# The other items' results of an attention and mixture-of-experts kernel: by blocks of 128 tokens in place of half items

## The chip, the cores and the metric

The kernel runs on one core of a Trainium2 chip. The metric is the device time of one execution in microseconds; the median of three executions of the kernel before is 2456.7 us (2454.43, 2456.7 and 2459.62). One more execution was recorded with the hardware profiler: it took 2459.43 us, of which the profile shows a span of 2457.7 us. All line numbers and rows are of that execution.

The engines are named as the profile names them: PE (TensorE, matrix products and transposes), PEld (its loads of weights), DVE (VectorE), ACT (ScalarE), POOL (GpSimd; here it issues the indirect DMAs that gather and scatter rows), SP (SyncE; here it issues the plain DMAs). Each engine takes its instructions in order, and waits on semaphores for those of others.

## The reference

The input is x of 8 items, each 256 channels by 1024 positions (32 by 32), float32. Two layers follow each other.

- Layer 0, on tokens (1024 by 256 in an item): `qkv = xt @ w_qkv + b_qkv`, 8 heads of 64, `attn = softmax(q k^T * 64**-0.5)` over the queries, `res = attn v`, then `res @ w_out + b_out + xt`.
- Layer 1: `t = t + attention(ln(t))` with one head and one matrix, `scores = (x W^T) x^T`, `y = softmax(scores) x`; then `t = t + moe(ln(t))`.
- The mixture of experts: `probs = softmax(tokens @ router_w.T)`, the two largest of 8 are kept and scaled to the sum 1, `out = tokens + sum over e of combine[:, e] * (gelu(tokens @ w1[e] + b1[e]) @ w2[e] + b2[e])`.

The result goes back to the layout of x: channels by positions.

## The kernel before

**The order of the whole.** Items 0 to 7 are computed one after the other. P is 128, D is 256, and an item has NT = 8 blocks of 128 tokens. Items 0 to 6 each go through layer 0, `attend` (the attention of layer 1), `normed` (the second layer norm and the router's products) and `dispatch`, which scatters each token's row to the places of its two experts; the item's tokens t2, with the norm already added to them, are stored to `sums` in memory. Before an item ends, the loads and first products of the next item's layer 0 are filled into its waits (`begun.at`). When layer 0 of item 7 is done, `experts` runs all experts' rows of items 0 to 6 in 63 blocks of 256 rows and writes the results to `y` in memory. What is left then is item 7 itself, and the collecting of the other seven items' results. The two are woven into each other, and this is the part that the change touches.

**Item 7.** `attend` runs eight steps, one for each block of 128 tokens: on PE the scores ps (L633, 128 by 1024), on DVE the negated maximum nmax (L641), on ACT the exponentials ex (L644), on PE eight transposes pa (L652), on DVE the copy aT (L654), on PE the product py (L659), on DVE L664, which scales py and adds it to t. The scores of later blocks are computed ahead. `normed` follows: layer norm on DVE (L217 to L224), transposes pt_n on PE (L233), copies n2T on DVE (L234), on POOL the addition of the norm to t (L775), and on PE the router's products pl (L687). Then `dense` computes all 8 experts for all tokens of item 7, since with one item there is nothing to sort: 16 steps, each with products pdh (L1164) and pdy (L1188) and the additions of pdy to t on DVE (L1197); the experts' weights come by plain DMAs (L1114, L1118).

**The results of items 0 to 6** (class `Results`). Each token has two rows in `y`, one for each of its experts. For an item and a half of its blocks (a "portion", 14 in all), eight indirect DMAs on POOL (L1053) fetch 128 rows of 256 numbers each into a tile yk; there are two such tiles, which share the tag xT. The item's `sums` are loaded into a tile o by SP (L1080). Eight instructions on DVE (L1085, `scalar_tensor_tensor`: row times gate plus o) add them. When an item's two halves are added, `store` transposes o on PE (pout, L1102, 8 for each of two channel halves of 128), copies each half on ACT to a tile oT (L1104), and SP writes it to the output (L1105).

**The places of that work.** The order on each engine is the order in which the program issues instructions, moved by a scheduler within what the dependences allow; `tc.issue_after(mixed.ins)` puts what follows behind the named DVE instruction. One `step()` is the whole of a portion: the store of an item that is complete, eight additions in a row, and the release of the eight gathers of the portion after next, which can start when DVE has read the yk tile that they overwrite. Two portions are begun ahead of `attend`. Which step of item 7 carries how many such steps is a table in the main loop, for the eight blocks of `attend` and the sixteen steps of `dense`:

```
early = {1: 1, 2: 1, 3: 1, 5: 1, 6: 1, 7: 1}
late = {0: 2, 3: 1, 4: 1, 6: 1, 8: 1, 9: 1, 11: 1, 12: 1}
```

In the changed kernel the same lines stand a few lines further on: L664 becomes L666, L654 L656, L641 L643, L687 L688, L775 L776; the gathers are at L1093, the additions at L1115, pout at L1152, oT at L1154, pdh at L1214 and pdy at L1238.

## Time and profile before

| | |
|---|---|
| times of three executions | 2454.43, 2456.7, 2459.62 us |
| the profiled execution | 2459.43 us, span 2457.7 us |
| PE busy | 97% of the span |
| DVE, ACT, POOL busy | 61%, 39%, 16% |
| chain of work that ended last | PE 90%, DVE 3%, ACT 2%, issue 2%, DMA 1%, another core or an unknown queue 1% |
| attention of an item (first L618 to end of last L664) | items 0 to 6 74.93 us each, item 7 105.6 us |
| from there to the first pl | items 0 to 6 8.02 us, item 7 8.96 us |
| gathers of results (L1053) | 112, mean 1048 ns, from 2193.6 us to 2419.4 us |
| additions of results (L1085) | 112, median 480 ns, 2226.7 to 2428.6 us |

How to read the rows. A group's line names its line in the program, the engine, the operation, the output and inputs by their names in the program, their sizes and the number of instructions, then the busy time, the mean of one, and the idle time of the engine just before them with what ended most of it. In a list in order of time the first two numbers are the start and the duration in us, and a bracket holds the idle time before it and what released it. "issue" stands for time in which the engine waited for nothing that the profile shows, "remote" for a release that the profile can't put down to an engine of this core. The busy time of matrix products is modelled at their ends. The clock is that which TensorE was granted, 1.00 being full speed. Matrix products in a row overlap, so a row's end can lie up to 0.2 us behind the next row's start.

### The profile page before, as it was taken

The page shows a single profiled execution, that of the slowest core. Times are in us where ns is not written, and L with a number is a line of the kernel's source. Part 1 is how long each engine was busy: PE and PEld are TensorE (multiplying, and loading weights), DVE is VectorE, ACT ScalarE, POOL GpSimd, SP SyncE. Part 2 cuts the span into 40 slices and gives each one's busy share as a digit, 9 for nine tenths or more (in the row PEclk, how much of TensorE's full clock was granted, in tenths as well). Part 3 has the DMA queues.
Part 4 walks back from the last instruction along what each step waited for, and adds up shares of the span by engine and source line. Part 5 has one row for each costly group of instructions (what it writes and reads, how often), then busy time and mean ns, then how long its engine had stood idle before and what let it go on. Part 6 is the DMA issues. An engine that isn't in the chain of part 4 may idle for free.

```text
span 2457.7 us, 37143 instructions
## 1 busy us (share of the span) xinstructions
PE 2386.2 (97%) x14015; PEld 1323.8 (54%) x14015; DVE 1497.3 (61%) x3642; ACT 953.5 (39%) x1587; POOL 391.1 (16%) x383
## 2 busy tenths in 40 slices
PE   9999999999999999999999999999999999997798
PEld 3356435654465346534653466346633788874466
DVE  5674677557746775577557755775578643334443
ACT  3651365136613661266126612662166222211222
POOL 0000011001100110011000100010002244444461
PEclk9999999999999999999999999999999999998799
DMA  7993101000100000000000000000002366652362
GB/s 280 386 376 83 35 18 36 1 18 19 35 1 18 19 19 17 18 16 21 18 18 14 23 18 18 10 27 1 18 7 74 116 208 223 208 173 91 99 196 91
DMA packets 82556, 188.23 MB, mean 77 GB/s; under 512 B 13992, under 2 KB 23880, under 8 KB 80584
## 3 DMA queue, kind: packets, MB, share of 16 engines
q1 hardware_dynamic: 57368, 118.65, 13.4%
q0 software_dynamic: 25008, 67.20, 8.7%
q8 instruction: 111, 1.82, 0.3%
q14 instruction: 69, 0.57, 0.1%
HBM read 100.49 MB, written 110.90 MB: 86 GB/s over the span
## 4 chain that ended last, share of the span: by engine, by line
PE 90%; DVE 3%; ACT 2%; issue 2%; DMA 1%; another core or an unknown queue 1%; SPq 0%; ACTq 0%; DVEq 0%; POOLq 0%
PE psc L420 18%; PE po L497 18%; PE py L659 9%; PE ps L633 7%; PE pqk L322 7%; PE pr L599 4%; PE pv L359 4%; PE ph L981 4%; PE pe L1006 4%; PE pdy L1188 2%; PE pdh L1164 2%; PE px L618 2%; PE pqk L300 2%; PE pa L652 2%
## 5 line engine op out<-in xcount | busy, mean ns | idle before, releaser
L461 ACT ACTIVATE ex<-psc,nmax 128x1024 f32<-128x1024 f32 x512 | 570.5, 1115 | 304.3 <-DVE scrap L444 221.8
L420 PE MATMUL psc<-qk,qk 64*64 64x512 f32 x4096 | 574.7, 592 | 4.3 <-ACT ex L461 4.3
L497 PE MATMUL po<-ex,vs 64*64 64x512 f32 x4096 | 570.2, 591 | 3.8 <-DVE vs L477 3.0
L444 DVE TENSOR_SCALAR_CACHE_REDUCE scrap<-psc,nmax 128x512 f32<-128x512 f32 x512 | 384.5, 751 | 178.4 <-PE psc L420 151.3
L435 DVE TENSOR_REDUCE nmax<-psc 128x1 f32<-128x512 f32 x512 | 350.8, 685 | 9.3 <-PE psc L420 9.3
L420 PEld LDWEIGHTS psc<-qk,qk 64*64 64x64 f32 x4096 | 179.8, 132 | 279.9 <-ACT ex L461 133.0
L497 PEld LDWEIGHTS po<-ex,vs 64*64 64x64 f32 x4096 | 175.3, 132 | 273.4 <-DVE vs L477 80.3
L659 PE MATMUL py<-n,aT 128*128 128x256 f32 x1024 | 244.4, 393 | 19.0 <-DVE aT L654 14.9
L659 PEld LDWEIGHTS py<-n,aT 128*128 128x128 f32 x1024 | 195.9, 195 | 84.5 <-DVE aT L654 53.8
L633 PE MATMUL ps<-nT,xa 128*128 128x512 f32 x512 | 236.5, 592 | 0.0
L844 POOL DMA_INDIRECT rows<-n,d_at x112 | 109.2, 975 | 705.5 <-DVE nmax L435 703.0
L644 ACT ACTIVATE ex<-ps,nmax 128x1024 f32<-128x1024 f32 x64 | 71.3, 1115 | 354.4 <-DVE nmax L641 338.6
L775 POOL TENSOR_TENSOR t<-t,n 128x2048 f32<-128x2048 f32 x8 | 36.3, 4535 | 1031.8 <-issue 766.8
L664 DVE SCALAR_TENSOR_TENSOR t<-py,rs,t 128x256 f32<-128x256 f32 x64 | 31.0, 484 | 234.9 <-PE py L659 197.8
L322 PE MATMUL pqk<-xT,wqkv 128*128 128x512 f32 x384 | 171.2, 599 | 0.0
L1053 POOL DMA_INDIRECT yk<-y,yat x112 | 117.4, 1048 | 120.9 <-DVE o L1085 72.2
L633 PEld LDWEIGHTS ps<-nT,xa 128*128 128x128 f32 x512 | 93.6, 190 | 79.9 <-issue 73.6
L322 PEld LDWEIGHTS pqk<-xT,wqkv 128*128 128x128 f32 x384 | 71.0, 190 | 99.9 <-issue 77.8
L287 ACT ACTIVATE qk<-pqk,b_qks 128x512 f32<-128x512 f32 x124 | 85.6, 691 | 96.1 <-PE pqk L322 79.8
L359 PE MATMUL pv<-wqkv,xT 128*128 128x512 f32 x256 | 119.6, 596 | 0.1
L641 DVE TENSOR_REDUCE nmax<-ps 128x1 f32<-128x1024 f32 x64 | 78.3, 1224 | 59.1 <-PE ps L633 58.6
L599 PE MATMUL pr<-wo,res 128*128 128x256 f32 x512 | 111.8, 379 | 0.0
(193 smaller groups left out, 2494.1 us busy)
## 6 DMA issues: line engine op xcount, KB each, us to landing
rows<-wb SPq DMA_DIRECT2D x7, 8192.0 KB
y<-yb SPq DMA_DIRECT2D x63, 256.0 KB
xT<-in_x_dram SPq DMA_DIRECT2D x7, 1024.0 KB
sums<-t SPq DMA_DIRECT2D x7, 1024.0 KB
o<-sums SPq DMA_DIRECT2D x7, 1024.0 KB
out_dram<-oT SPq DMA_DIRECT2D x14, 512.0 KB
wpack<-in_L_ffn_w_dram SPq DMA_DIRECT2D x4, 1024.0 KB
wb<-in_L_ffn_w_dram SPq DMA_DIRECT2D x16, 256.0 KB
```

Of the source, the lines that this page charges most:

```text
L322: mm = nc.tensor.matmul(pq[:, ts(n, 512)], wqkv[:, cc, t, ts(g, P)], xT[:, cc, ts(n, 512)], start=(cc == 0), stop=(cc == NCC - 1),)
L359: nc.tensor.matmul(pv, self.xT[:, cc, ts(i, P)], wqkv[:, cc, 2, :], start=(cc == 0), stop=(cc == NCC - 1),)
L420: mm = nc.tensor.matmul(pss[at, h][ts(c, DK), ts(n, 512)], k[r, j * P + c * DK : j * P + (c + 1) * DK], q[r, ts(n, 512)], start=True, stop ...
L435: firsts[at, h] = nc.vector.tensor_reduce(nmax, pss[at, h][:, ts(0, 512)], AX.X, ALU.max, negate=True)
L444: seconds[h] = nc.vector.tensor_scalar(scrap, pss[at, h][:, ts(1, 512)], -1.0, nmaxes[at, h], ALU.mult, ALU.min, accum_out=nmax,)
L461: nc.scalar.activation(ex, pss.pop((at, h)), AF.Exp, bias=nmaxes.pop((at, h)), scale=1.0, accum_out=sums[at][:, h : h + 1],)
L497: mm = nc.tensor.matmul(po[n][ts(h, DK), :], vss[at][keys, h, :], exps[at, h][keys, ts(n, 512)], start=(j == 0 and turn == 0), stop=(j == ...
L599: nc.tensor.matmul(pr[:, :C], res[:, g, ts(i, P)], wo[:, g, :], start=(g == 0), stop=(g == NPAIR - 1))
L633: nc.tensor.matmul(psc[:, ts(n, 512)], xa[:, ec, ts(i, P)], nT[:, ec, ts(n, 512)], start=(ec == 0), stop=(ec == NCC - 1),)
L659: nc.tensor.matmul(py[:, :D], aT[:, ts(m, P)], n1[:, m, :], start=(m == 0), stop=(m == NT - 1))
L844: scatter = nc.gpsimd.indirect_dma_start(out=view[:, :], out_offset=bass.IndirectOffsetOnAxis(ap=ats[k][:, i : i + 1], axis=0), in_=n2[:, ...
L1053: nc.gpsimd.indirect_dma_start(out=yk[:, i, k, :], out_offset=None, in_=self.group.y[:, :], in_offset=bass.IndirectOffsetOnAxis(ap=ats[k][ ...
```

## The change

The unit of the collecting becomes one block of 128 tokens: two gathers and two additions; there are 56 units. The two yk tiles are allocated once and used as a ring of eight slots, a unit in each. A table PLACES says for many more places of item 7 how many units are added there, how many are let go to POOL, and how many channel halves are stored. The places are DVE instructions of `attend` (the copies xa, the maxima, L666), `normed`, the gates and the steps of `dense`. A unit that is let go gets a dependence on the DVE instruction of its place ("behind"), so that POOL waits for it. A unit is added some two places after it is let go. In `attend` 22 of the 56 units are added, three at most places; none is added at the last block. A store is one channel half. The tiles o hold two items, and the next item's sums are loaded when the second block of an item is added. The counts of gathers, additions, loads of sums, transposes, copies and output DMAs stay what they are.

As the scheduler places them, five additions stand between L666 and the next copy aT, and a sixth behind the copy; the addition on POOL (L776) stands behind 60 of the 112 gathers; the four channel halves of items 0 and 1 are transposed before the last product py.

```diff
--- before.py
+++ after.py
@@ -221,9 +221,10 @@
         nc.scalar.activation(rstd, rstd, AF.Sqrt)
         nc.vector.reciprocal(rstd, rstd)
         for i in range(NT):
-            nc.vector.tensor_scalar(
+            written = nc.vector.tensor_scalar(
                 dst[:, i, :], t[:, i, :], mv[:, i, 0:1], rstd[:, i : i + 1], ALU.subtract, ALU.mult
             )
+        return written
 
     def to_channels(t, dst, name):
 
@@ -231,7 +232,8 @@
             pt = big(f"pt_{name}_{cc}")
             for i in range(NT):
                 nc.tensor.transpose(pt[:, ts(i, P)], t[:, i, ts(cc, P)], ident)
-            nc.vector.tensor_copy(dst[:, cc, :], pt)
+            copied = nc.vector.tensor_copy(dst[:, cc, :], pt)
+        return copied
 
     def prepare():
 
@@ -387,7 +389,7 @@
             assert len(self.todo) == 2
             self.values(2, single=True)
 
-    def nothing(_):
+    def nothing(*_):
         pass
 
     def layer0(b, xT, begun, routing):
@@ -603,7 +605,7 @@
         return t1
 
 
-    def attend(b, t1, fill, step=nothing):
+    def attend(b, t1, fill, tick=nothing):
         n1 = one.tile([P, NT, D], F32, tag="n", name=f"n1_{b}")
         layer_norm(t1, n1, 1e-5, f"a{b}")
         fill("norm 1")
@@ -622,7 +624,7 @@
                         start=(dc == 0),
                         stop=(dc == NCC - 1),
                     )
-            nc.vector.tensor_copy(xa[:, ec, :], px)
+            tick(("xa", ec), nc.vector.tensor_copy(xa[:, ec, :], px))
 
         t2 = t1
 
@@ -638,7 +640,7 @@
                         stop=(ec == NCC - 1),
                     )
             nmax = small.tile([P, 1], F32, tag="nmax", name=f"nmax_{b}_{i}")
-            nc.vector.tensor_reduce(nmax, psc, AX.X, ALU.max, negate=True)
+            tick(("max", i), nc.vector.tensor_reduce(nmax, psc, AX.X, ALU.max, negate=True))
             ex = expp.tile([P, 1024], F32, tag="exps", name=f"ex1_{b}_{i}")
             ssum = small.tile([P, 1], F32, tag="ssum", name=f"ssum_{b}_{i}")
             nc.scalar.activation(ex, psc, AF.Exp, bias=nmax, scale=1.0, accum_out=ssum)
@@ -664,8 +666,7 @@
             mixed = nc.vector.scalar_tensor_tensor(
                 t2[:, i, :], py[:, :D], rs, t1[:, i, :], ALU.mult, ALU.add
             )
-            with tc.issue_after(mixed.ins):
-                step(i)
+            tick(("mixed", i), mixed)
 
         pending = None
         for i in range(NT):
@@ -764,13 +765,13 @@
 
     groups = [Group(n, items) for n, items in enumerate(GROUPS)]
 
-    def normed(b, t2, fill):
+    def normed(b, t2, fill, tick=nothing):
 
         n2 = one.tile([P, NT, D], F32, tag="n", name=f"n2_{b}")
-        layer_norm(t2, n2, 1e-5, f"f{b}")
+        tick("normed", layer_norm(t2, n2, 1e-5, f"f{b}"))
         fill("norm 2")
         nT = one.tile([P, NCC, S], F32, tag="nT", name=f"n2T_{b}")
-        to_channels(n2, nT, f"n2_{b}")
+        tick("turned", to_channels(n2, nT, f"n2_{b}"))
 
         nc.gpsimd.tensor_add(t2, t2, n2)
         fill("normed 2")
@@ -1036,67 +1037,116 @@
 
 
 
+        SLOTS = 8
+        PLACES = {
+            **{("xa", ec): (0, 1, 0) for ec in range(2)},
+            ("max", 0): (0, 1, 0),
+            **{("max", i): (0, 1, 0) for i in range(1, 8)},
+            ("mixed", 0): (4, 2, 0),
+            **{("mixed", i): (3, 2, 0) for i in range(1, 7)},
+            "last weights": (0, 0, 2),
+            "last products": (0, 0, 1),
+            ("mixed", 7): (0, 2, 0),
+            "norm 2": (0, 0, 1),
+            "normed": (0, 2, 0),
+            "turned": (3, 2, 0),
+            "gates": (3, 2, 0),
+            ("dense", 0): (3, 2, 2),
+            ("dense", 1): (3, 2, 0),
+            **{("dense", k): (2, 2, 2) for k in range(2, 16)},
+        }
+
         def __init__(self, group):
             self.group = group
-            self.portions = [(b, half) for b in group.items for half in range(2)]
-            self.rows = {}
-            self.done = 0
-            self.total = None
-
-        def gather(self, at):
-            b, half = self.portions[at]
-            ats = self.group.kept[b][1]
-            yk = two.tile([P, NT // 2, 2, D], F32, tag="xT", name=f"yk_{b}_{half}")
-            for i in range(NT // 2):
-                for k in range(2):
-                    block = half * (NT // 2) + i
-                    nc.gpsimd.indirect_dma_start(
-                        out=yk[:, i, k, :],
-                        out_offset=None,
-                        in_=self.group.y[:, :],
-                        in_offset=bass.IndirectOffsetOnAxis(
-                            ap=ats[k][:, block : block + 1], axis=0
-                        ),
-                    )
-            self.rows[at] = yk
+            self.units = [(b, i) for b in group.items for i in range(NT)]
+            self.yks = [
+                two.tile([P, self.SLOTS // 2, 2, D], F32, tag="xT", name=f"yk_{n}")
+                for n in range(2)
+            ]
+            self.sent, self.added = 0, 0
+            self.pairs, self.totals = [], []
+            self.whole = []
+
+        def slot(self, at):
+            return self.yks[at // (self.SLOTS // 2) % 2][:, at % (self.SLOTS // 2)]
+
+        def load(self, n):
+
+            b = self.group.items[n]
+            if n % 2 == 0:
+                self.pair = one.tile(
+                    [P, 2, NT, D], F32, tag=("v", "res")[n // 2 % 2], name=f"o_{b}"
+                )
+            self.totals.append(self.pair[:, n % 2])
+            nc.sync.dma_start(self.totals[n], self.group.sums[n])
+
+        def gather(self, behind=None):
+            at = self.sent
+            if at == len(self.units):
+                return
+            assert at < self.added + self.SLOTS
+            self.sent += 1
+            b, i = self.units[at]
+            for k in range(2):
+                ins = nc.gpsimd.indirect_dma_start(
+                    out=self.slot(at)[:, k, :],
+                    out_offset=None,
+                    in_=self.group.y[:, :],
+                    in_offset=bass.IndirectOffsetOnAxis(
+                        ap=self.group.kept[b][1][k][:, i : i + 1], axis=0
+                    ),
+                )
+                if behind is not None:
+                    tc.add_manual_dep(ins.ins, behind.ins.name, BEHIND)
+
+        def add(self):
+            at = self.added
+            if at == len(self.units):
+                return
+            assert at < self.sent
+            self.added += 1
+            b, i = self.units[at]
+            n = at // NT
+            gate = self.group.kept[b][0]
+            total = self.totals[n]
+            for k in range(2):
+                nc.vector.scalar_tensor_tensor(
+                    total[:, i, :],
+                    self.slot(at)[:, k, :],
+                    gate[:, k, i : i + 1],
+                    total[:, i, :],
+                    ALU.mult,
+                    ALU.add,
+                )
+            if i == 1 and n + 1 < len(self.group.items):
+                self.load(n + 1)
+            if i == NT - 1:
+                self.whole += [(b, total, cc) for cc in range(NCC)]
 
         def begin(self):
-            for at in range(2):
-                self.gather(at)
-
-        def step(self):
-            at = self.done
-            self.done += 1
-            if at % 2 == 0 and at > 0:
-                store(self.portions[at - 1][0], self.total, range(NT))
-            if at == len(self.portions):
-                return
-            b, half = self.portions[at]
-            gate = self.group.kept[b][0]
-            if half == 0:
-                self.total = one.tile(
-                    [P, NT, D], F32, tag=("v", "res")[at // 2 % 2], name=f"o_{b}"
-                )
-                nc.sync.dma_start(self.total, self.group.sums[self.group.items.index(b)])
-            yk = self.rows.pop(at)
-            for i in range(NT // 2):
-                block = half * (NT // 2) + i
-                for k in range(2):
-                    nc.vector.scalar_tensor_tensor(
-                        self.total[:, block, :],
-                        yk[:, i, k, :],
-                        gate[:, k, block : block + 1],
-                        self.total[:, block, :],
-                        ALU.mult,
-                        ALU.add,
-                    )
-            if at + 2 < len(self.portions):
-                self.gather(at + 2)
-
-    def store(b, total, blocks):
+            self.load(0)
+            for _ in range(2):
+                self.gather()
+
+        def tick(self, place, behind=None):
+            added, sent, stored = self.PLACES.get(place, (0, 0, 0))
+            if added:
+                with tc.issue_after(behind.ins):
+                    for _ in range(added):
+                        self.add()
+            for _ in range(sent):
+                self.gather(behind)
+            for _ in range(stored):
+                if self.whole:
+                    b, total, cc = self.whole.pop(0)
+                    store(b, total, range(NT), [cc])
+
+    def store(b, total, blocks, ccs=range(NCC)):
 
         n = len(blocks)
-        for cc in range(NCC):
+        for cc in ccs:
             pt = big(f"pout_{b}_{blocks[0]}_{cc}")
             for at, i in enumerate(blocks):
                 nc.tensor.transpose(pt[:, ts(at, P)], total[:, i, ts(cc, P)], ident)
@@ -1106,7 +1156,7 @@
                 out[b, ts(cc, P), blocks[0] * P : (blocks[0] + n) * P], oT[:, : n * P]
             )
 
-    def dense(b, t2, step):
+    def dense(b, t2, tick):
 
 
         def weights(e):
@@ -1124,7 +1174,7 @@
         nc.sync.dma_start(b2_rows, b2)
         for e in range(NWB):
             weights(e)
-        _, nT, l = normed(b, t2, nothing)
+        _, nT, l = normed(b, t2, tick, tick)
         routing = gates(b, l)
         while True:
             try:
@@ -1137,7 +1187,7 @@
         second = small.tile([P, NT, E], F32, tag="d_rows", name=f"second_{b}", bufs=1)
         nc.vector.tensor_mul(all_gates, hots[0], bcast(gate[:, 0], E))
         nc.vector.tensor_mul(second, hots[1], bcast(gate[:, 1], E))
-        nc.vector.tensor_add(all_gates, all_gates, second)
+        tick("gates", nc.vector.tensor_add(all_gates, all_gates, second))
 
         def biases():
 
@@ -1202,8 +1252,7 @@
                         ALU.mult,
                         ALU.add,
                     )
-            with tc.issue_after(added.ins):
-                step(e * NH2 + n)
+            tick(("dense", e * NH2 + n), added)
             if n == NH2 - 1 and e + NWB < E:
                 weights(e + NWB)
             if e == E - 1:
@@ -1238,17 +1287,9 @@
         experts(groups[0])
         others = Results(groups[0])
         others.begin()
-
-        early = {1: 1, 2: 1, 3: 1, 5: 1, 6: 1, 7: 1}
-        late = {0: 2, 3: 1, 4: 1, 6: 1, 8: 1, 9: 1, 11: 1, 12: 1}
-
-        def step(where, at):
-            for _ in range(where.get(at, 0)):
-                others.step()
-
-        t2 = attend(b, t1, nothing, lambda i: step(early, i))
-        dense(b, t2, lambda i: step(late, i))
-        assert others.done > len(others.portions)
+        t2 = attend(b, t1, others.tick, others.tick)
+        dense(b, t2, others.tick)
+        assert others.added == len(others.units) and not others.whole
 
 
 # ---- launch: one core; inputs and outputs as the reference has them ----
```

## The prediction

> **What bounds the kernel now.** I read the page first (shares of the engines, the slices, the costly groups), then the waits of TensorE behind 2100 us, then tables of stretches, then rows. TensorE is busy for 97% of the span; what it loses lies in the last 270 us, where the diff works.
>
> ```profile
> PE 2386.2 (97%) x14015; PEld 1323.8 (54%) x14015; DVE 1497.3 (61%) x3642; ACT 953.5 (39%) x1587; POOL 391.1 (16%) x383
> L1053 POOL DMA_INDIRECT yk<-y,yat x112 | 117.4, 1048 | 120.9 <-DVE o L1085 72.2
> ```
>
> TensorE has work almost throughout, and the 112 gathers of 1.048 us run on POOL. Next a table of stretches: the attention of item 6, from its first L618 to the end of its last L664, and that of item 7, the same code with gathers, additions and stores woven in (columns: length, then PE, PEld, DVE, ACT and POOL busy, granted clock).
>
> ```profile
> 1690.66:1765.59 74.93, 74.47 (x284) 47.64 (x283) 32.94 (x52) 12.21 (x18) 0.00 (x0) 1.00 0.00 1
> 2189.24:2294.83 105.59, 83.95 (x304) 54.65 (x304) 46.15 (x90) 14.78 (x21) 53.11 (x54) 0.89 0.36 113
> ```
>
> Item 7 takes 30.66 us more for as much TensorE work: 21.6 us idle, and a clock of 0.89. The waits of TensorE in 2100 to 2460 us (sum, times, longest) give the places:
>
> ```profile
> PE py L659 <- DVE aT L654: 14.9, 3, 8.3
> PE pdy L1188 <- issue: 7.1, 3, 4.4
> PE pl L687 <- DVE n2T L234: 6.6, 1, 6.6
> PE pt_n L233 <- DVE n L224: 5.4, 1, 5.4
> PE py L659 <- issue: 4.1, 1, 4.1
> ```
>
> VectorE is named, but its rows say that it waited too, for something that is no engine's work:
>
> ```profile
> 2216.20 0.48 DVE L664 SCALAR_TENSOR_TENSOR t<-py,rs,t 128x256 f32<-128x256 f32 x1 [10.27 <-remote]
> 2253.03 0.48 DVE L664 SCALAR_TENSOR_TENSOR t<-py,rs,t 128x256 f32<-128x256 f32 x1 [11.70 <-remote]
> ```
>
> TensorE's own rows show the product that the first of these needs, done at 2209.46, and the stalls after it:
>
> ```profile
> 2205.74 3.72 PE L659 MATMUL py<-n,aT 128*128 128x256 f32 x16
> ...
> 2219.66 5.92 PE L659 MATMUL py<-n,aT 128*128 128x256 f32 x13 [5.88 <-DVE aT L654]
> ```
>
> So L664 began 6.7 us after its operand's end. POOL's rows say what went on: 16 gathers without a break, 1.26 us apart, of which the last is
>
> ```profile
> 2212.51 0.96 POOL L1053 DMA_INDIRECT yk<-y,yat  x1 [0.30 <-issue]
> ```
>
> It ends at 2213.47, and L664 starts 2.7 us later. All the others are alike: runs of gathers end at 2250.63, 2308.08 and 2360.31; VectorE goes on at 2253.03 (py_3 was done at 2244.56), 2310.83 (pt_n at 2303.76) and 2361.67 (pdy at 2354.64). In a run of 8 gathers (2256.95 to 2266.72) nothing was late; in the long ones it began between the 8th and the 17th gather. I read: **during a long unbroken run of gathers TensorE's completions reach the others only when the run ends.** The cause is not in the profile. TensorE then idles, and its clock falls (same columns as the first table):
>
> ```profile
> 2253.00:2259.00 6.00, 0.00 (x0) 0.00 (x0) 5.97 (x12) 1.15 (x2) 1.74 (x2) 0.50 0.22 83
> 2259.00:2265.00 6.00, 6.00 (x18) 4.73 (x19) 0.77 (x4) 0.06 (x1) 4.47 (x6) 0.67 0.34 100
> 2311.00:2322.00 11.00, 9.89 (x28) 4.24 (x29) 5.63 (x26) 4.59 (x7) 1.62 (x1) 0.70 0.00 0
> ```
>
> **The change part by part.** Totals stay: 112 gathers, 112 additions, 14 half stores, 7 loads of sums. What moves is their place.
>
> Runs of gathers. Before, one step releases 8, and two steps' worth can stand in a row. Now a unit is 2 gathers, each held by the VectorE instruction named with it: four gathers per L666 (the old L664) and two per maximum, 6 in a step of attention, 4 in a step of the dense layer. A step of attention is 7.88 us (item 6: rows of L659 at 1739.54 and 1747.42), 6 gathers are 6 × 1.26 = 7.56: POOL is nearly full there, but it can't run ahead, since a late L666 releases nothing. In the dense layer 4 × 1.26 = 5.04 us of a step of 6.89 (8 pdh from 2365.00 to 2368.43, 16 pdy to 2371.89) leave a gap in every step.
>
> Additions. Before, 8 in a row (3.25 us) stand after L664 and, at the end, ahead of something urgent: aT (2283.12 to 2286.28, TensorE waits 4.1 us) and the layer norm (2294.75 to 2297.91, 5.4 us). Now five stand between L666 and the copy aT, one behind it. VectorE then has aT ready at 0.48 + 5 × 0.41 + 1.21 = 3.7 us after a product, while TensorE has pa (0.87) and ps (3.43) = 4.3 us to do: hidden, with 0.6 us to spare. After products 5 and 6 no ps is left: TensorE has pa, pa and two half stores (3.5) against 3.9, and then two half stores (1.75) against 3.97 (with 0.25 for the signals): 0.4 + 2.2 us exposed. None stands any more between the last L666 and the layer norm.
>
> Sum against the profiled execution (2459.43):
> - Attention of item 7 if nothing disturbs it: 74.93, less item 6's two value fills (3.46), plus four half stores (32 × 0.109 = 3.5), plus 2.6 exposed = 77.6. Gain 105.6 − 77.6 = 28.0.
> - But the first run: 12 gathers are let go by 2204.5 (4 at the start, 4 at xa, 4 at the maxima), so POOL works to 2208.7 without a break, and by the lag of 2.7 the first L666 starts at 2211.4 instead of 2209.5: +2.0.
> - POOL beside additions: the 112 gathers took 117.4 where 112 × 0.957 = 107.2, so an addition costs POOL 10.2 / 112 = 0.09 us; a step of POOL is then 7.56 + 0.55 = 8.1, 0.2 too long, 1.4 over six steps. By the costliest group (a gather of 4.04 beside 8 additions, 3.1 over) it is 6/8 × 3.1 = 2.3 a step, 2.0 too long, 12 over six steps, less some 5 that a unit is released ahead of its addition: 7. Bounds 0 and 7; I take 2.0, by the mean, with something for the last steps.
> - Norm: the 8 additions go, −3.2.
> - The copy n2T's wait, −6.6; the half clock after it (2311 to 2322 at 0.70, 0.30 × 9.89), −3.0.
> - Dense layer: waits −7.1 (1.73 + 0.99 + 4.38), half clock (2398 to 2402 at 0.50: 1.8; 2385 to 2398 at 0.93: 0.5), −2.3.
> - One late completion left somewhere after the attention (ten gathers and the 4.5 us addition of L776 stand close around the norm): bounds 0 and 8.3 (the longest wait above), I take 4: +4.
> - SyncE: sums are fetched per item as before, into pairs of tiles; the load of item 4 waits for the transposes of items 0 and 1, which stand ahead of py_7, that of item 6 for a store three dense steps earlier. Each is ordered a step ahead of its additions; nothing. If that cover were gone, the additions behind it, and in order all of VectorE, wait for one 1 MB load.
> - Stores one channel half at a time: the same 16 + 16 transposes and two copies per two halves; a half is 0.87 us in place of 1.75. TensorE reads sums whose additions VectorE finished a step earlier: nothing; if one is late, it is the 0.7 to 1.1 us that pout waits now.
>
> Sum: −28.0 + 2.0 + 2.0 − 3.2 − 6.6 − 3.0 − 7.1 − 2.3 + 4 = −42.2, so 2417.2. The profiled execution is 2.7 above the median of the three (2456.7), so on that scale **2414.5 us**.
>
> A rule against the change: additions, each reading two operands in SBUF, now stand beside gathers in every step. Row: an addition took 474 to 485 ns in all 112 cases, gathers or not, while gathers beside additions took up to 4.04 us instead of 0.96; so VectorE loses nothing and POOL a little, which is the sum above. The Trainium skill ("SBUF — State Buffer", section "Who interferes with whom") says that such an instruction contends with a GpSimd instruction that reads SBUF, the second to issue being fully blocked. By it each of five additions could stand behind a gather of 0.96, some 4.8 us a step, six steps +25, 2440 (an estimate). The rows contradict the half of it that would hurt.
>
> **The rivals.**
> - B: the completions stay late in attention. For: POOL is busy 7.56 of 7.88, so its gathers can still form runs of twelve and more; the first is certain. Against: a stuck L666 releases nothing, POOL runs dry after at most 6 gathers. Price: up to 7.6 + 2.7 less 4.3 of cover, about 6, plus a slow product (5.68 or 6.75 against 3.72, about 2.5) = 8.5; 56 gathers give room for three such runs, less the 2.0 + 4 already in the sum: +19.5, 2434.
> - C: POOL gets too slow. If two of six gathers in a step are like the six longest beside additions (1.22, 1.28, 1.68, 2.07, 3.73, 4.04; mean 2.34), a step is 4 × 1.26 + 2 × 2.64 = 10.3, 2.4 too long, 14.6 over six steps; less 5 of lead, +9.6: 2424.
> - D, the other side: additions wait for gathers ahead of aT in every step, and TensorE with them. If all six gathers of a step took 2.34 + 0.30, a step is 15.8, 7.9 too long; six steps +48: 2462. It turns slower where it eats 42, that is 7 us a step, from 14.9 / 6 − 0.30 = 2.2 us a gather on. Against: only six of 112 gathers were long, most at the start of a group of additions.
> - E: the late completions have a cause other than the runs (say the number of outstanding transfers), so that the same total of gathers gives the same waits, while additions still leave the path: −3.2 − 4.1 and little else: 2449.
>
> **How the numbers follow.** Chances: forecast 0.48 (2402 to 2424: with the three allowances at nothing it is 2406.5, with the exposed 2.6 hidden too 2404, less 2 for the spread of runs; with 7 and 8.3 for the two that have bounds 2424), B 0.27, C 0.09, E 0.06, D 0.07, no change 0.03. The range 2402 to 2446 takes in A to C and B with one run more (+8.5). 0.2% (4.9 us) is what a measurement of this kernel tells from no change. Faster: 0.48 + 0.27 + 0.09 + 0.06 = 0.90, same 0.03, slower 0.07.
>
> **What would show it.** Right: item 7's attention near 82 us; few long waits of L666 put down to a remote releaser; a clock of 1.00 in attention; the wait of pl and those of pdy gone; the gathers' idle time before them spread over VectorE's releases. B: L666 rows with 5 us and more and a clock of 0.5 to 0.7 after. C and D: additions (L1115) that wait for transfers, and gathers well over 1.1 us in the mean. Wrong altogether: long runs gone, and the completions late as before.

## The result, and the profile after

The kernel after takes 2432.98 us (median of six executions, 2432.29 to 2433.64), the kernel before, on the same chip, 2455.78 us (six executions, 2454.43 to 2459.62). The ratio is 0.9905, with a 95% interval from 0.9893 to 0.9918: 22.8 us faster. The prediction had 2414.5 us with a range from 2402 to 2446; the time lies inside the range, and about 1 us from rival B (2434), not at the forecast. The profiled execution took 2433.04 us, its span is 2431.3 us.

Three stretches hold all that changed: the attention of item 7, from its end to the router's first product pl, and the rest. The table of stretches of the kernel before has, for the second and the third (columns: start and end, length, then busy time of PE, PEld, DVE, ACT and POOL, the granted clock, the DMA share and GB/s):

```profile
2294.83:2303.79 8.96, 4.02 (x16) 2.84 (x16) 7.96 (x22) 0.21 (x1) 6.58 (x7) 0.63 0.31 89
2303.79:2457.70 153.91, 135.40 (x522) 90.36 (x522) 61.27 (x158) 36.01 (x51) 62.23 (x53) 0.93 0.39 124
```

and that of the kernel after, for all three:

```profile
2188.71:2280.17 91.46, 77.15 (x304) 51.11 (x304) 48.53 (x94) 14.77 (x21) 50.56 (x52) 0.94 0.37 112
2280.17:2286.22 6.05, 3.93 (x17) 2.47 (x17) 5.01 (x15) 0.21 (x1) 4.56 (x5) 0.83 1.01 415
2286.22:2431.30 145.08, 135.95 (x522) 91.12 (x522) 65.45 (x162) 36.03 (x51) 57.86 (x57) 0.95 0.38 121
```

| stretch | before | after | change | predicted change |
|---|---|---|---|---|
| attention of item 7 | 105.59 | 91.46 | −14.1 | −24.0 (−28.0 + 2.0 + 2.0) |
| to the first pl | 8.96 | 6.05 | −2.9 | −3.2 |
| first pl to the end | 153.91 | 145.08 | −8.8 | −15.0 (−6.6 − 3.0 − 7.1 − 2.3 + 4) |
| span | 2457.7 | 2431.3 | −26.4 | −42.2 |

(0.5 us more went ahead of the attention, in the part that the change doesn't touch.) TensorE's waits after 2100 us, the view that gave the places of loss before, have other names now:

```profile
PE pa L654 <- ACT oT L1154: 7.0, 1, 7.0
PE py L661 <- DVE aT L656: 4.0, 3, 1.8
PE py L661 <- issue: 2.7, 1, 2.7
PE pt_n L234 <- DVE n L224: 2.5, 1, 2.5
PE pg L1196 <- DVE all_gates L1190: 2.5, 1, 2.5
PE plT L711 <- ACT lT L696: 2.1, 1, 2.1
```

The wait of pl behind n2T (6.6 us) and those of pdy (7.1) are gone, pt_n waits 2.5 instead of 5.4, and py 6.7 instead of 19.0. New are pa, pg and plT. What stands behind pa and py shows in the rows of VectorE (start, duration, and in the bracket the idle time before and its releaser):

```profile
2222.82 1.23 DVE L656 COPY aT<-pa 128x1024 f32<-128x1024 f32 x1 [0.62 <-remote]
...
2227.10 1.22 DVE L643 TENSOR_REDUCE nmax<-ps 128x1 f32<-128x1024 f32 x1 [2.11 <-remote]
...
2242.76 1.22 DVE L656 COPY aT<-pa 128x1024 f32<-128x1024 f32 x1 [2.52 <-issue]
...
2261.29 1.23 DVE L656 COPY aT<-pa 128x1024 f32<-128x1024 f32 x1 [2.53 <-remote]
```

of POOL (the last gather of a run of twelve that began at 2247.13):

```profile
2261.22 0.95 POOL L1093 DMA_INDIRECT yk<-y,yat  x1 [0.30 <-issue]
```

and of ACT and PE, one fence each:

```profile
2264.15 1.93 ACT L1154 COPY oT<-pout 128x1024 f32<-128x1024 f32 x2 [8.95 <-remote]
```

```profile
2256.33 1.91 PE L1152 MATMUL pout<-ident,o 128*128 128x128 f32 x16
2265.21 1.76 PE L654 MATMUL pa<-ident,ex 128*128 128x128 f32 x7 [6.97 <-ACT oT L1154]
2266.76 5.47 PE L661 MATMUL py<-n,aT 128*128 128x256 f32 x16
```

The reader is to see the pattern of before once more. The transposes pout are done at 2258.2, the run of gathers ends at 2262.17, and ACT starts copying at 2264.15, 2.0 us after the run's end and 5.9 after its operand. TensorE had to wait for that copy's buffer, its clock fell (0.62 from 2265.2 to 2272.2 us), and the next py took 5.47 us instead of 3.72. The rows of aT at 2242.76 and 2261.29 came some 4.8 us after their transposes, each 14.2 us after the beginning of a run of twelve. So the change did shorten the long runs, from 16 to 24 gathers down to 12, but in attention there are still four runs of twelve, and behind the eight gathers ahead of POOL's addition L776 the copy lT is late as well (TensorE's plT waits 2.1 us).

### The profile page after: what moved, and what is told of

It reads as the page before. It is cut to its first block, busy times and chain, and to the rows that moved or that the text cites. A ratio compares the mean times of both kernels' runs of the same rounds, so it can differ in the third digit from the quotient of the medians.

```text
span 2431.3 us, 37154 instructions
## 1 busy us (share of the span) xinstructions
PE 2380.9 (98%) x14015; PEld 1320.7 (54%) x14015; DVE 1499.5 (62%) x3642; ACT 952.8 (39%) x1587; POOL 381.4 (16%) x383
## 3 DMA queue, kind: packets, MB, share of 16 engines
q1 hardware_dynamic: 57368, 118.65, 13.5%
## 4 chain that ended last, share of the span: by engine, by line
PE 91%; DVE 3%; ACT 2%; issue 1%; DMA 1%; another core or an unknown queue 1%; SPq 0%; ACTq 0%; DVEq 0%; POOLq 0%
PE psc L422 18%; PE po L499 18%; PE py L661 9%; PE ps L635 7%; PE pqk L324 7%; PE pr L601 5%; PE pv L361 4%; PE ph L982 4%; PE pe L1007 4%; PE pdy L1238 2%; PE px L620 2%; PE pqk L302 2%; PE pa L654 2%; PE pdh L1214 2%; PE pt_n L234 1%
## 5 line engine op out<-in xcount | busy, mean ns | idle before, releaser
L661 PE MATMUL py<-n,aT 128*128 128x256 f32 x1024 | 238.4, 386 | 6.8 <-DVE aT L656 4.0
L776 POOL TENSOR_TENSOR t<-t,n 128x2048 f32<-128x2048 f32 x8 | 36.3, 4535 | 1032.0 <-issue 766.8
L666 DVE SCALAR_TENSOR_TENSOR t<-py,rs,t 128x256 f32<-128x256 f32 x64 | 30.9, 483 | 206.3 <-PE py L661 206.3
L1093 POOL DMA_INDIRECT yk<-y,yat x112 | 108.5, 969 | 108.4 <-DVE t L1247 39.5
```

The lines of the kernel that those rows point to most:

```text
L661: nc.tensor.matmul(py[:, :D], aT[:, ts(m, P)], n1[:, m, :], start=(m == 0), stop=(m == NT - 1))
L1093: ins = nc.gpsimd.indirect_dma_start(out=self.slot(at)[:, k, :], out_offset=None, in_=self.group.y[:, :], in_offset=bass.IndirectOffsetOnAxis(
```

## Experiments

The theory at this point: during an unbroken run of gathers, from about the eighth on, TensorE's completions reach the other engines late, and after are let through some 2 us behind the run's end; what is left of the loss in attention is that. Rivals: the additions ahead of aT; the transfers themselves rather than their issuing; a busy POOL; the stores' own chain. The runs fell on several chips; each group below ran on one chip, beside the kernel before on that chip.

### Four ways to take one suspect away (the kernel before took 2460.3 there)

Half of the gathers:

```diff
-            for k in range(2):
+            for k in range(1):
                 ins = nc.gpsimd.indirect_dma_start(
...
-                    self.slot(at)[:, k, :],
+                    self.slot(at)[:, 0, :],
                     gate[:, k, i : i + 1],
```

> Leaves out the second gather of each unit (both additions read the first one's rows): 56 gathers in place of 112, three in a step of attention, additions as before. Theory (completions of TensorE come late in long unbroken runs of gathers): three gathers are 3.8 us of a step of 7.9, no run passes 6, so item 7's attention falls from 91.5 us to 77 to 80, the copies aT and the copies oT wait for nothing remote, and the whole is 2412 to 2420. Rival (the additions ahead of aT): attention stays at 88 us or more. Both: the slow stretch around the gates stays as long as additions stand there.

No additions:

```diff
-            for k in range(2):
-                nc.vector.scalar_tensor_tensor(
...
-                )
             if i == 1 and n + 1 < len(self.group.items):
```

> Leaves out all 112 additions (the sums are stored without the experts' rows); the gathers stay at their places and in their number. Theory of the runs: the runs stay as long, so attention stays at 86 to 92 us, with late copies aT. Rival (additions): attention 77 to 80. At the gates both expect the wait of pg to shrink by some 2 us, as the addition of 2.32 us is gone.

The same bytes by plain DMAs of SyncE:

```diff
-                ins = nc.gpsimd.indirect_dma_start(
...
-                )
+                ins = nc.sync.dma_start(
+                    self.slot(at)[:, k, :], self.group.y[(2 * at + k) * P : (2 * at + k + 1) * P, :]
+                )
```

> In place of each gather a plain DMA on SyncE that fetches 128 rows of y that lie in a row (wrong rows, same bytes, same releases); POOL then has only its addition in item 7. Theory of the runs (POOL's issuing of gathers): nothing is late, attention 77 to 80 us, whole 2412 to 2420. Rival (the traffic of the transfers, or their number outstanding, holds the completions up): attention stays at 88 or more with the same late copies.

POOL busy, but without a DMA:

```diff
-                ins = nc.gpsimd.indirect_dma_start(
...
-                )
-                if behind is not None:
-                    tc.add_manual_dep(ins.ins, behind.ins.name, BEHIND)
+                for _ in range(2):
+                    ins = nc.gpsimd.memset(self.slot(at), 0.25)
+                    if behind is not None:
+                        tc.add_manual_dep(ins.ins, behind.ins.name, BEHIND)
```

> In place of each gather two memsets on POOL over the unit's slot (wrong values), some 1.1 us by the 0.21 us that a memset of 128 by 128 takes here, with the same releases: POOL is as busy, nothing is transferred. If POOL being busy is enough to hold the completions up, attention stays at 88 or more; if it needs the gathers' DMAs, it is 77 to 81 us.

Measured: 2415.06, 2423.12, 2410.73 and 2417.9 us, one execution each. The line of item 7's attention in the four tables of stretches, half of the gathers first:

```profile
2190.16:2266.51 76.35, 73.77 (x304) 49.41 (x304) 48.24 (x94) 14.79 (x21) 26.46 (x26) 1.00 0.30 90
```

no additions:

```profile
2190.17:2272.28 82.11, 76.25 (x304) 50.37 (x304) 32.14 (x50) 12.68 (x19) 49.70 (x52) 0.98 0.39 117
```

plain DMAs by SyncE:

```profile
2189.72:2266.08 76.36, 73.76 (x304) 49.42 (x304) 48.24 (x94) 14.78 (x21) 0.00 (x0) 1.00 0.41 129
```

memsets on POOL:

```profile
2190.00:2266.35 76.35, 73.76 (x304) 49.42 (x304) 48.23 (x94) 14.79 (x21) 47.61 (x96) 1.00 0.15 49
```

Three of the four give 76.35 us, to a hundredth (just under the 77 us at which the expected ranges began), with a clock of 1.00 and no row of VectorE or ACT that waits for a remote releaser. That is the attention undisturbed; 91.46 in the kernel after is 15.1 us more. A POOL that is as busy (47.6 us) does nothing to it; its unbroken stretches are shorter there, one of 13.5 us (with no pause over 0.6 us) and the others of 6.4 at most, where twelve gathers take 15, but in the one of 13.5 us nothing was late either. The same bytes at 129 GB/s through another queue do nothing to it. Half of the gathers, with the same additions and the same stores, is enough to lose the whole 15.1: there no run is longer than three. So neither the additions nor the stores are the cause, and the rival of the traffic falls as well, as far as plain transfers go. Half of the gathers also means fewer of them, not only shorter runs; the paced kernel below comes back to that.

Without additions the late completions are there still: of the runs of POOL, four have twelve gathers, and the copy aT that ought to follow at once comes late,

```profile
2258.40 1.23 DVE L656 COPY aT<-pa 128x1024 f32<-128x1024 f32 x1 [2.77 <-remote]
```

and L666 before it 5.09 us (remote). But they cost 5.8 us against 76.35 (the undisturbed length without additions was not measured), not the 10 to 15 that the expectation had (86 to 92): both numbers on record, that of the theory and that of its rival (77 to 80), missed. Where six additions have to be done between a late aT and the next step, a late completion costs more than where VectorE has nothing else to do; that this makes the difference of 9.3 us is argued, not shown.

### Places changed, on a chip that surprised

Two units a step instead of three ("paced"):

```diff
-            **{("xa", ec): (0, 1, 0) for ec in range(2)},
-            ("max", 0): (0, 1, 0),
-            **{("max", i): (0, 1, 0) for i in range(1, 8)},
-            ("mixed", 0): (4, 2, 0),
-            **{("mixed", i): (3, 2, 0) for i in range(1, 7)},
+            ("xa", 0): (0, 1, 0),
+            **{("max", i): (0, 1, 0) for i in range(8)},
+            **{("mixed", i): (2, 1, 0) for i in range(7)},
             "last weights": (0, 0, 2),
-            "last products": (0, 0, 1),
-            ("mixed", 7): (0, 2, 0),
-            "norm 2": (0, 0, 1),
-            "normed": (0, 2, 0),
-            "turned": (3, 2, 0),
-            "gates": (3, 2, 0),
-            ("dense", 0): (3, 2, 2),
-            ("dense", 1): (3, 2, 0),
-            **{("dense", k): (2, 2, 2) for k in range(2, 16)},
+            ("mixed", 7): (0, 1, 0),
+            "normed": (0, 1, 0),
+            "turned": (2, 1, 0),
+            "gates": (2, 2, 0),
+            ("dense", 0): (3, 3, 2),
+            **{("dense", k): (2 + (k + 1) % 2, 2 + (k + 1) % 2, 2) for k in range(1, 6)},
+            **{("dense", k): (3 - k % 2, 3 - k % 2, 2) for k in range(6, 16)},
```

> Nothing is left out; only the table of places differs. In the attention of item 7 two units a step are let go (one at the maximum, one at L666) and two added, in place of three; the dense layer takes three and two in turn. POOL's share of a step of attention falls to 4 x 1.26 = 5.04 of 7.8 us. Theory of the runs: attention 76 to 79 us in place of 91.5, no late completion there; in the dense layer runs of 6 to 10 gathers come up, which may cost 0 to 5. Whole 2415 to 2423. If what counts is not the length of a run but the gathers' total, attention stays at 85 or more and the whole at 2426 or more.

No addition between n2T and the gates:

```diff
-            "turned": (3, 2, 0),
-            "gates": (3, 2, 0),
+            "turned": (0, 0, 0),
+            "gates": (6, 4, 0),
```

> The kernel after, but the three units that are added behind the copy n2T are added behind the gates, with the three there, and the releases of the two places go together: no addition between n2T and the gates. Reading: one addition there took 2.32 us beside POOL's addition L776, pg waited 2.5 us, and TensorE then ran at half clock for 16 us (pb 7.19 for 4.00 us). Expected: that addition's 2.32 is gone, pg waits 1 us or less, 2427 to 2431. Rival: the gates are late through the late copy lT (2.1 us) alone, or the clock falls anyway: 2432 to 2434, no change.

Stores later:

```diff
-            "last weights": (0, 0, 2),
-            "last products": (0, 0, 1),
...
-            "norm 2": (0, 0, 1),
```

> The kernel after, but no half store in the attention or at the norm; the four go to the dense layer. Theory of the runs: the longest wait (7.0 us at pa behind oT) gets shorter but not away, as the copy aT_6 was late too (2261.3); attention 91.5 less 3.5 of transposes, less some 4 of that wait: 81 to 87; the dense layer gets the 3.5 back: whole 2425 to 2430. Rival (the stores' own chain, transposes, copy oT, its buffer, is the cause): attention 75 or less, whole 2418 to 2422.

Paced, and no addition between n2T and the gates (against the paced table):

```diff
-            "turned": (2, 1, 0),
-            "gates": (2, 2, 0),
+            "turned": (0, 1, 0),
+            "gates": (4, 2, 0),
```

> The places of the paced kernel and, as well, no addition between n2T and the gates (two units more behind the gates). If the two causes are apart, both gains add up: the paced kernel's time less what the gates-first kernel gains, 2411 to 2419; if the slow clock behind the gates comes from elsewhere, the paced kernel's time.

Measured: 2419.22 (five executions), 2414.31, 2416.90 and 2414.35 us (four each). But the kernel before took 2429.57 us there (eight executions, 2427.57 to 2430.39), 25 to 31 less than in the other groups and in the first result; the ratios to it are 0.9961 (0.9946 to 0.9975), 0.9943 (0.9927 to 0.9960), 0.9955 (0.9938 to 0.9972) and 0.9934 (0.9918 to 0.9951). The gates-first kernel lets its gathers go in attention exactly as the kernel after does, and its attention is undisturbed:

```profile
2187.99:2264.34 76.35, 73.77 (x304) 49.43 (x304) 48.30 (x94) 14.78 (x21) 51.52 (x52) 1.00 0.44 134
```

although POOL, as nothing is late, runs through 36 gathers from 2209.0 to 2255.3 without a break. On this chip long runs do no harm. So the runs alone are not the whole cause; something that differs between chips, or between their states at the time, belongs to it. The four kernels therefore say nothing here on pacing or on the stores as a remedy (the stores-later kernel had 72.40 us of attention: 76.35 less 3.5 for its four half stores, and 0.4 more), and the expectations for those two could not be tested. What they do test is the gates, since the paced kernel with and without that edit differ by 4.9 us.

The row that explains it is the one of L776, POOL's addition of 4.52 us over two operands in SBUF. In the kernel after it, and the addition on VectorE beside it, read

```profile
2290.34 4.51 POOL L776 TENSOR_TENSOR t<-t,n 128x2048 f32<-128x2048 f32 x1
```

```profile
2292.82 2.32 DVE L1115 SCALAR_TENSOR_TENSOR o<-yk,gate,o 128x256 f32<-128x256 f32 x1
2295.07 0.20 DVE L719 TENSOR_REDUCE g_m<-g_l 128x8 f32<-128x64 f32 x1
```

L776 ends at 2294.85; the addition, which takes 0.48 us elsewhere, ends at 2295.14, and the gates' chain behind it waits. In the gates-first kernel no addition stands there, but the gates' own subtraction, 64 numbers a partition and 0.23 us elsewhere, falls into the same trap:

```profile
2274.42 4.52 POOL L776 TENSOR_TENSOR t<-t,n 128x2048 f32<-128x2048 f32 x1
```

```profile
2274.47 4.57 DVE L721 TENSOR_TENSOR g_p<-g_l,g_m 128x64 f32<-128x64 f32 x1
```

so that pg waited 4.7 us there, not the 1 us or less that was expected. In the kernel without additions the subtraction took 1.51 us beside L776, so that the wait of pg fell only from 2.5 to 1.7 us and not by the 2 us expected. In the half-gathers, the memset and the paced kernels an addition beside L776 took 4.33, 4.73 and 4.63 us. In the paced kernel with the gates first, L776 has ended when the gates' subtraction starts (0.23 us), and pg waits 0.4 us where it waits 3.5 in the paced kernel. This is what the Trainium skill states ("SBUF — State Buffer", section "Who interferes with whom"): a VectorE instruction with two inputs in SBUF contends with a GpSimd instruction that reads SBUF, and the second to issue is blocked until the first has finished. Where the VectorE instruction started second, rows and rule agree to 0.3 us. In the stores-later kernel a VectorE instruction of the gates with two operands in SBUF (L727) started 0.29 us ahead of L776, by the rows, and took 4.89 us all the same; there the order of the starts doesn't fit the rule.

### The kernels before and after on a third chip

Both unchanged.

> The kernel before, unchanged, for its trace beside the kernel after on one chip: on the chip of the last four runs it took 2427 to 2430 us in place of 2454 to 2460. Theory: the late completions depend on the chip. Where the time is about 2429, its L664 rows have no remote waits and item 7's attention is about 80 us, 25 less than in the first profile; where it is about 2456 they stand as before. If instead the 26 us lie elsewhere (in layer 0 or in the experts), the attention stays at 105 us in either case.

> The kernel after, unchanged, on the same chip as the kernel before. Where the chip shows late completions: 2431 to 2435 against 2455 to 2460, as in the first result. Where it shows none: attention 76.4 us, as the gates-first kernel had with the same places there, so 2414 to 2420, against 2429; the gain is then 10 to 15 us, from the additions' places (norm, aT) and the slow clock behind them alone.

Measured: before 2458.53 us (seven executions beside them; the profiled one 2458.68), after 2432.19 us (four), ratio 0.9894 (0.9875 to 0.9914). This chip shows the late completions, with the first result's numbers. The stretches of before and of after:

```profile
2189.72:2293.21 103.49, 83.83 (x304) 54.66 (x304) 46.20 (x90) 14.78 (x21) 52.69 (x54) 0.88 0.37 115
```

```profile
2189.82:2280.11 90.29, 78.51 (x304) 52.19 (x304) 48.64 (x94) 14.88 (x21) 51.01 (x52) 0.94 0.37 113
```

So the result repeats. One thing in this trace of before doesn't fit late completions alone. In its run of 24 gathers, from 2335.53 to 2368.53, TensorE issued products one by one, 1.4 to 2.8 us apart, with nothing that the profile shows to wait for:

```profile
2363.46 0.52 PE L1188 MATMUL pdy<-wb,dh 128*128 128x256 f32 x1 [2.41 <-issue]
2364.89 0.59 PE L1188 MATMUL pdy<-wb,dh 128*128 128x256 f32 x1 [0.91 <-issue]
2366.29 0.58 PE L1188 MATMUL pdy<-wb,dh 128*128 128x256 f32 x1 [0.82 <-issue]
```

The waits of pdy put down to issue are 7.3 us in all here and were 7.1 in the prediction's list. So in a long run TensorE's own instructions can come slowly too; what holds them up is open. On the chip without late completions the kernel after was not run; that its gain there would be smaller follows for the part that the late completions have in it, but its size is open.

### Pacing where completions are late

The paced kernel and the paced kernel with the gates first, on the third chip again.

> The paced kernel once more (two units a step in attention, three and two in the dense layer; nothing left out), hoping for a chip on which the kernel before takes 2454 to 2460 us and its completions come late. There the kernel after takes 2432, its attention 90 to 91.5. Theory of the runs: attention 77 to 79 as on the other chip, whole 2417 to 2424, ratio to before 0.984 to 0.987. If pacing does nothing against late completions: attention 85 or more, whole 2427 or more. On a chip without late completions the run repeats 2419.

> The paced kernel with no addition between n2T and the gates, once more, beside the paced one. On a chip with late completions: some 5 us under the paced kernel, as it was on the other chip (2419.2 and 2414.4), so 2412 to 2419, the best of the kernels that compute the whole. If the copy lT and the gates are late there whatever stands on VectorE, no difference to the paced kernel.

Measured: 2422.5 us (2420.37 to 2425.11) and 2417.28 us (2416.67 to 2421.54), four executions each, with before at 2454.12 (six, 2451.97 to 2459.10): ratios 0.9864 (0.9842 to 0.9885) and 0.9843 (0.9824 to 0.9862). Both lie under the kernel after on the same chip (0.9894, 0.9875 to 0.9914): the intervals of the second don't touch, those of the first overlap in a small part. The attention of the paced kernel:

```profile
2188.26:2265.74 77.48, 73.54 (x288) 48.74 (x288) 41.85 (x78) 12.85 (x19) 34.41 (x36) 0.98 0.30 91
```

It is 77.48 us on the chip with late completions and was 77.49 on the one without, against 90.3 of the kernel after. Behind a first run of eight, its runs in attention hold four gathers at most, some of them only 1 us apart. With the half gathers this is the second piece of evidence that breaking the runs takes the late completions away, and nothing is left out here. But it also lets fewer gathers go in the attention, 36 in place of 52, so their number might be what counts. The dense layer in the same trace speaks against that. There 66 gathers go in 100.45 us, more to the us than the kernel after's 52 in 91.46, in runs of four, six and ten, and TensorE is idle for 1.7 us in all:

```profile
2301.10:2401.55 100.45, 98.78 (x381) 66.22 (x380) 50.47 (x122) 24.66 (x35) 66.03 (x66) 1.00 0.58 188
```

The gates give 5.2 us more (4.9 on the other chip), with pg's wait down from 3.4 to 0.6 us.

In the dense layer three and two units a step make runs of ten, and in the second kernel one of fourteen. The first kernel has no row there that waits for a remote releaser; the second has some, behind one of its three runs of ten and behind the fourteen. Its rows of POOL (the last gather of each of the two runs) and of VectorE and ACT behind them:

```profile
2339.62 0.95 POOL L1089 DMA_INDIRECT yk<-y,yat  x1 [0.30 <-issue]
...
2385.74 0.95 POOL L1089 DMA_INDIRECT yk<-y,yat  x1 [0.30 <-issue]
```

```profile
2342.42 1.66 DVE L1243 SCALAR_TENSOR_TENSOR t<-pdy,all_gates,t 128x256 f32<-128x256 f32 x4 [6.05 <-remote]
2389.22 1.66 DVE L1243 SCALAR_TENSOR_TENSOR t<-pdy,all_gates,t 128x256 f32<-128x256 f32 x4 [6.33 <-remote]
```

```profile
2389.03 1.93 ACT L1150 COPY oT<-pout 128x1024 f32<-128x1024 f32 x2 [11.41 <-remote]
```

The runs end at 2340.57 and 2386.69, the others go on 1.85 and 2.3 us later. On the chip without late completions the same kernel's last stretch took 141.79 us, here 146.80 (each profiled execution was the slowest of its four): 3.2 us more of it are idle time of TensorE, 1.8 are busy time. So some 3 us more, at most, may be had by shorter runs in the dense layer too; that was not tried.

## Why the prediction was right, and where it was not

- **The mechanism.** The prediction's reading, that completions come late while gathers are issued without a break and that this is where the kernel lost its time, holds: half of the gathers and pacing remove it on chips that have it. Its phrase "only when the run ends" was too strong. In a run of twelve some are let through 14.2 us after its beginning, so a completion was held 5 to 6 us at most. The rows of before had that already: a copy oT (L1104) that waited for a remote releaser went on at 2244.50, 6.1 us before its run of sixteen ended.
- **Attention, −28.0.** The undisturbed attention was set at 77.6; it is 76.35, so the exposed 2.6 us at the last steps are 1.4 by the same sum (one wait of py behind aT, 1.8 us, is left in the undisturbed runs). This term was right to 1.3 us.
- **The allowances in attention, +2.0 for the first run and +2.0 for POOL: the step that failed.** They should have been 15.1 together. The prediction argued that "a late L666 releases nothing", so that POOL runs dry. It does, after 12 gathers; but twelve are enough to hold a completion for 5 us, and that happened in four runs. py waited 1.0, 1.2 and 2.7 us; the fourth time it fell on the half stores, and pa waited 7.0: 11.9 us together, and 3.4 by the slower clock (77.15 us busy for 73.77). That is rival B, with a chance of 0.27, and its reason, a POOL that is nearly full, was right: undisturbed, it ran 36 gathers without a break. Its price in attention, 19.5 us over the forecast, was too high (9.9), so that its 2434 was hit only with the 6.2 us that went behind the norm: that agreement is luck.
- **POOL beside additions.** The mean gather got shorter, 969 ns in place of 1048, and none over 1.28 us; the rivals C and D had no ground. The additions went at 478 ns.
- **Norm, −3.2:** −2.9.
- **n2T's wait, −6.6, and the waits of pdy, −7.1:** both gone in full.
- **The slow clock, −3.0 and −2.3:** not gained. TensorE's busy time in the last stretch rose from 135.40 to 135.95 us. The prediction costed nothing for the additions that now stand between n2T and the gates, which it named nowhere. One of them waits for L776 (2.3 us for 0.48), lT comes late (2.1 us), and pg waits 2.5 us; TensorE then ran at half clock to 2316, and pb took 7.19 us where it took 4.00. In sums: TensorE's idle time fell by 9.4 us (18.5 to 9.1) where 13.7 were expected, its busy time rose by 0.55 where a fall of 5.3 was; 10.2 less, of which the allowance covers 4. That a loss of this size hangs on the gates is shown by the paced kernel with and without additions ahead of them: 5 us apart on two chips. By the two traces from the chip without late completions, 3.1 us of it are idle and 2.2 busy time of TensorE. How long the clock stays low is not explained by the wait alone: the gates-first kernel waited 4.7 us at pg, and its clock was 0.60 for 4 us and 1.00 from then on, where the kernel after had 0.57 for 16 us.
- **The rule weighed against a row.** The prediction set the SBUF rule aside because no addition was slower than 485 ns beside gathers. For gathers that stands: also in the kernel after, five additions in a row take 2.06 us. But POOL had one instruction that does read SBUF, and the rows of before showed no addition beside it; there an addition ends with L776, as the rule has it, and the change put an addition there.
- **Rival E** (another cause than the runs) was half right in a way that the prediction had not thought of: the runs are needed, but on one chip they do nothing.

By sums: 15.1 − 4.0 in the allowances of attention, −1.25 in its undisturbed length, 0.3 at the norm and 6.2 behind it make 16.35, less 0.5 ahead of the attention: the 15.8 us between the predicted gain of the span (42.2) and the measured one (26.4).

## What to carry to other kernels

When an engine seems to wait for work that the rows show long done, look at what a third engine does at that moment: here it was gathers issued back to back by POOL. One run of eight and runs of four, with pauses between them, cost nothing where four runs of twelve cost 15 us. Spreading a burst is only half of it: count how many of the smaller pieces come to stand in a row again once they are let go at every step. And before an instruction with two operands in SBUF goes onto a path that matters, see whether POOL has a long instruction there that reads SBUF as well: in every such row here the short one ended within 0.3 us of the long one's end.

## What the runs showed of the hardware

- TensorE's completions reach VectorE and ACT up to 6 us late in a run of twelve gathers issued 1.26 us apart (up to 8.5 in one of sixteen, and a copy oT 14.9 in one of twenty-four). Some are let through within the run, the others 0.2 to 3.4 us behind its end. Of the paced kernels' seven runs of ten on the third chip one showed it clearly (oT 3.0 us late), and so did the eight gathers ahead of L776 (lT 2.7 us late); the other runs of eight that had a pause of several us before them, and those of six and fewer, delayed nothing by more than 1.3 us. Memsets on POOL in the same places (47.6 us of 76) and plain DMAs of the same bytes do not do it. What delays them is open: no row names it.
- In a run of twenty-four TensorE's own products came singly, 1.4 to 2.8 us apart, with no wait that the profile shows.
- It depends on the chip, or on its state: on one, 36 gathers in a row held nothing up, and the kernel before was 25 to 31 us faster there (2429.6 against 2454.1 to 2460.3 elsewhere). The attentions of items 0 to 6 take 74.93 us on all of them. Which property it is, is open.
- A VectorE instruction of 64 numbers a partition took 4.57 us, 20 times its 0.23, as POOL's 4.52 us addition had begun 0.05 us before it.
